# Zeros pad three small matrices of the mambas to 68 rows

## The chip, the cores and the metric

The kernel runs on one NeuronCore of a Trainium2 chip. The metric is the device time of one execution in microseconds, the median of several runs. The engines have short names in the profile: PE is the tensor engine (PEld its weight loads), DVE the vector engine, ACT the scalar engine, POOL the GpSimd engine, and SP the engine whose queue issues most of the DMA transfers. Each engine works through its own instructions in program order, and semaphores make them wait for each other.

## The reference

The program is a sequence of four layers on an image batch of 4 x 192 x 64 x 64 in float32. Layer 0 holds two mamba blocks on the same normalised input (the second sees its channels reversed), layer 1 one mamba block, followed by a depthwise convolution and an MLP. Layers 2 and 3 are a masked depthwise convolution with weights made from pooled channels, and windowed mixing with an MLP. The change touches the mambas only. Each of them computes, for every token,

```
xc, z = split(x @ in_w.T);  xc = silu(causal_conv(xc) + conv_b)
dbl = xc @ x_w.T                        # 12 + 16 + 16 = 44 values a token
dt = softplus(dbl[:12] @ dt_w.T + dt_b) # 384 channels
B, C = dbl[12:28], dbl[28:44]
h = exp(dt * A) * h + dt * xc * B       # 384 x 16 states
y = sum over states of h * C, + D * xc, times silu(z);  out = y @ out_w.T
```

There are 4096 tokens an image and 4 images. The 44 values a token, `dbl`, are what matters here: 12 of them give the step sizes `dt`, 16 are B and 16 are C.

## The kernel before

The tokens are cut into units of 512, 32 units for each mamba: 64 units in layer 0, where the two mambas alternate, and 32 in layer 1. Tiles are laid with channels on the partitions and 512 tokens along the free dimension. Float32 products are recorded as two passes each, a weight load and a matmul a pass.

A unit has a front and a scan. The front (`Mamba.front`) makes, one after the other: the input projection into `ps_in` (line 475, weights of 96 rows), the convolution as shifted diagonal matmuls into `ps_conv` (line 557, mambas of layer 0 only; layer 1 sums the taps with ACT and POOL), silu, then the x-projection into `ps_x` (line 493: three products accumulate 384 channels into 44 output partitions), a copy by ACT into the SBUF tile `dbl` (line 495), and the three products of `dt_w` with the first 12 rows of `dbl` into `ps_dt` (line 504), each evicted by ACT (line 507). Softplus follows, POOL multiplies `dt` with `xc`, and both go to DRAM, from where `load` (line 602) reads them back, each row repeated over 8 partitions.

The scan takes 12 groups of 128 (channel, state) pairs four times over. `spread` (line 609) and `spread_C` (line 625) multiply a matrix of zeros and ones with `dbl` and so repeat the rows of B and C over the partitions: each is a product with 44 contracted rows and 128 output columns, two for B and two for C a unit. ACT makes the decays `dA` (line 648), DVE or POOL the product of `dtxE` and B (line 641), DVE runs the scan (line 654), POOL multiplies with C (line 667), and PE gathers the sum over states into `y` (line 676). In the gather four products of 32 output columns each write four quarters of the partitions.

The order of the instructions on every engine is written out by a planner, `Behind`, before anything runs: the scans set the pace, and pieces of the fronts, of the norms and of the work after the scans are placed between them, by costs and dues given as constants in the code. Such a constant is not worked out from the sizes of the tiles. PSUM banks of the front rotate over two buffers, and one `dbl` is in use at a time.

Layers 2 and 3 start from the images of layer 1 and end the program; from about 8660 us on nothing but these runs.

Of the kernel before, what the change touches and what calls it, by code (L numbers as in the profile page):

```python
# [14 lines left out]
F32 = mybir.dt.float32  # L15
# [11 lines left out]
DI = 384  # L27
ND = DI // 128
NS = 16
RK = 12  # L30
HID = 768
NH = HID // 128
T = 512
# [21 lines left out]
class Pack:  # L55


    def __init__(self, parts):
        self.parts, self.arrays, self.at, self.width = parts, [], {}, 0
# [24 lines left out]
def chunked(a, p):  # L84

    a = a.reshape((a.shape[0] // p, p) + a.shape[1:])
    return np.moveaxis(a, 0, 1)
# [318 lines left out]
class Expand:  # L406
# [3 lines left out]


    def __init__(self, nc, const, spread_ap, gather_ap):
        self.spread = const.tile([RK + 2 * NS, 4, 128], F32, name="spread")
        nc.sync.dma_start(self.spread, spread_ap)
        self.gather = const.tile([128, 2, 32], F32, name="gather")
        nc.sync.dma_start(self.gather, gather_ap)


class Mamba:
# [3 lines left out]
    def __init__(  # L423
        self, nc, name, taps, ins, const, last, scan, work, psum_y, psum_a, dram, ident, ex, behind, shared=(),
        summed=False, xcs=3,
    ):

        self.behind, self.xcs, self.shared, self.summed = behind, xcs, shared, summed
        self.nc, self.name, self.taps, self.ex = nc, name, taps, ex
        self.last, self.work, self.psum_y, self.psum_a = last, work, psum_y, psum_a
        self.dram = dram
        pack, pack_ap, in_w_ap, dt_w_ap = ins
        t = const.tile([128, pack.width], F32, name=f"{name}_pack")
        nc.sync.dma_start(t, pack_ap)
        w = pack.views(t)
        self.in_w = scan.tile([CP, 2, 2 * DI], F32, name=f"{name}_in_w")
        nc.scalar.dma_start(self.in_w, in_w_ap)  # L440
        self.dt_w = scan.tile([RK, DI], F32, name=f"{name}_dt_w")
        nc.scalar.dma_start(self.dt_w, dt_w_ap)
        self.conv_b, self.dt_b, self.D = w["conv_b"], w["dt_b"], w["D"]
        self.x_w, self.out_w = w["x_w"], w["out_w"]
        self.A = scan.tile([128, NQ, 4], F32, name=f"{name}_A")
        nc.scalar.activation(self.A, w["A_log"], AF.Exp)
        nc.vector.tensor_scalar_mul(self.A, self.A, -1.0)
        self.conv_w = w["conv_w"]
        if not summed:
            self.conv = scan.tile([128, ND, taps, 128], F32, name=f"{name}_conv")  # L450
            for d in range(ND):
                for j in range(taps):
                    nc.vector.tensor_scalar_mul(
                        self.conv[:, d, j, :], ident, w["conv_w"][:, d, j : j + 1]
                    )
        if not summed:
            self.skip_w = scan.tile([128, ND, 128], F32, name=f"{name}_skip")
            for d in range(ND):
                nc.vector.tensor_scalar_mul(self.skip_w[:, d, :], ident, self.D[:, d : d + 1])
        self.halo = scan.tile([128, ND, taps if summed else taps - 1], F32, name=f"{name}_halo")  # L460
        self.state = scan.tile([128, NQ, 4], F32, name=f"{name}_state")

    def front(self, xn, first, u):


        nc, K, behind = self.nc, self.taps, self.behind
        raw = self.work.tile([128, ND, K - 1 + T], F32, name="raw", bufs=1)
        if first:
            nc.gpsimd.memset(self.halo, 0.0)
        nc.gpsimd.tensor_copy(raw[:, :, 0 : K - 1], self.halo[:, :, : K - 1])  # L470

        def projected(e):
            ps = behind.bank([128, T], "ps_in")
            for k in range(2):
                nc.tensor.matmul(  # L475
                    ps, self.in_w[:, k, bass.ts(e, 128)], xn[:, k, :], start=(k == 0), stop=(k == 1)
                )
            return ps

        def project(e, to):  # L480
            ps = projected(e)
            return behind.later(lambda: nc.scalar.copy(to, ps))  # L482

        if self.summed:
            yield from self.sum_taps(raw, projected, u)
        else:
            yield from self.convolve(raw, project, u)
        xc = u["xc"]
        nc.scalar.activation(xc, xc, AF.Silu)  # L489
        yield Piece(2.6, bank=True, wait=2 if self.summed else 4)  # L490
        ps = behind.bank([RK + 2 * NS, T], "ps_x")
        for d in range(ND):
            nc.tensor.matmul(ps, self.x_w[:, d, :], xc[:, d, :], start=(d == 0), stop=(d == ND - 1))  # L493
        dbl = u["dbl"] = self.work.tile([RK + 2 * NS, T], F32, name="dbl", bufs=1)
        h = behind.later(lambda ps=ps: nc.scalar.copy(dbl, ps))  # L495
        halves = []
        for d in range(ND):
            yield Piece(0.85, bank=True, after=[h], wait=0 if d else 3)
            if d == 0:
                dt = self.work.tile([128, ND, 1 + T if self.summed else T], F32, name="dt", bufs=1)  # L500
                dt = dt[:, :, :T]
                dtx = raw[:, :, K - 1 :]
            ps = behind.bank([128, T], "ps_dt")
            nc.tensor.matmul(ps, self.dt_w[:, bass.ts(d, 128)], dbl[:RK, :], start=True, stop=True)  # L504
            halves.append(
                behind.later(
                    lambda d=d, ps=ps: nc.scalar.activation(
                        dt[:, d, :], ps, AF.Identity, bias=self.dt_b[:, d : d + 1]
                    )
                )  # L510
            )
        yield Piece(after=halves, burst=True, act=4.1)
        nc.scalar.activation(dt, dt, AF.Softplus)  # L513
        nc.gpsimd.tensor_tensor(dtx, dt, xc, ALU.mult)  # L514
        rows = []
        for i, v in enumerate((dt, dtx)):
            yield Piece(wait=1 + i)
            r = self.dram.tile([DI, T], F32, name=("r_dt", "r_dtx")[i], bufs=3)
            nc.sync.dma_start(r.rearrange("(c p) t -> p c t", p=128), v)
            rows.append(r)  # L520
        yield Piece(1.7, bank=True, after=u["z_free"])
        u["rows"] = rows
        z = u["z"] = self.work.tile([128, ND, T], F32, name="z", bufs=2)
        made = []
        for d in range(ND):
            if d:
                yield Piece(1.7, bank=True)
            made.append(project(ND + d, z[:, d, :]))

        def silu():  # L530
            nc.scalar.activation(z, z, AF.Silu)
            u["silu"] = True
            yield Piece()

        said = Piece(after=made, burst=True, act=4.1)
        if self.summed:
            behind.add(4, silu(), said)
        else:
            yield said
            yield from silu()  # L540
# [1190 lines left out]
def scan_order(a):  # L1731

    a = a.reshape(ND, 4, 2, 16, 2, 8)
    return a.transpose(3, 5, 0, 2, 4, 1).reshape(128, NQ, 4)


def scan_matrices():
    spread = np.zeros((RK + 2 * NS, 4, 16, 8), np.float32)
    for o in range(4):
        for n in range(8):  # L1740
            spread[RK + 8 * o + n, o, :, n] = 1.0
    gather = np.zeros((16, 8, 2, 2, 16), np.float32)
    for q in range(2):
        for dd in range(16):
            gather[dd, :, q, q, dd] = 1.0
    return spread.reshape(RK + 2 * NS, 4, 128), gather.reshape(128, 2, 32)


def laid_out(inputs):

    arrays, packs = {}, {}

    def mamba(name, in_w, conv_w, conv_b, x_w, dt_w, dt_b, A_log, D, out_w):
        p = packs[name] = Pack(128)
        for n, a in (
            ("conv_w", conv_w),
            ("conv_b", conv_b),
            ("dt_b", dt_b),
            ("D", D),
            ("A_log", scan_order(A_log)),  # L1760
            ("x_w", x_w.T),
            ("out_w", out_w.T),
        ):
            p.add(n, a if n == "A_log" else chunked(a, 128))
        arrays[f"{name}_in_w"] = chunked(in_w.T, CP)
        arrays[f"{name}_dt_w"] = dt_w.T

    order = ["in_w", "conv_w", "conv_b", "x_w", "dt_w", "dt_b", "A_log", "D", "out_w"]
    m1 = [inputs[f"L0_conv_m1_{n}"] for n in order]
# [7 lines left out]

    i = {k[len("L1_conv_") :]: v for k, v in inputs.items() if k.startswith("L1_conv_")}
    mamba(
        "m",  # L1780
        i["in_proj_w"],
# [42 lines left out]
    arrays["sed"] = paired(np.moveaxis(i["w_sed"], 0, 1))[:, :2]  # L1824

    arrays["spread"], arrays["gather"] = scan_matrices()
    for n, p in packs.items():
        arrays[n] = p.array()
# [18 lines left out]
```

## Time and profile before

| | |
|---|---|
| median of 3 runs | 10563.82 us (10560.6 to 10564.75) |
| span of the profiled execution | 10559.3 us |
| PE busy | 8657.5 us, 82% of the span |
| DVE busy | 8765.6 us, 83% |
| POOL busy | 7932.4 us, 75% |
| ACT busy | 6675.7 us, 63% |
| mean granted PE clock | 0.860 |
| `ps_x` (line 493), 128 rows, 44 columns | 576 passes, 592 / 598 / 1084 ns (shortest, median, longest) |
| `ps_dt` (line 504), 12 rows, 128 columns | 576 passes, 587 / 692 / 1219 ns |
| `B` (line 609), 44 rows, 128 columns | 384 passes, 588 / 693 / 1220 ns |
| `ps_C` (line 625), 44 rows, 128 columns | 384 passes, 588 / 590 / 1220 ns |

A row of the profile names the line, engine and operation, what is written and read, and the form: "44*128 44x512" is a weight of 44 rows and 128 columns, and 44 partitions of 512 moving elements. A matmul's own duration holds its way through the array, which overlaps the next one; what a pass takes from PE is the distance between starts. The clock row gives the share of the full PE clock that was granted. In a table by stretches each column is an engine's busy time in that stretch, then the clock, the share of the DMA engines' time and their rate. In a line of waits the three numbers are the total in us, how often, and the longest.

### The profile page before, as it was taken

The numbers are of one execution on the slowest core, as the hardware profiler recorded it, in microseconds if no ns is written. First come the engines' busy times: TensorE is split into PE (matmuls) and PEld (weight loads), VectorE is DVE, ScalarE is ACT, GpSimd is POOL, SyncE is SP. The second block draws the span as 40 slices with busy tenths as digits, with TensorE's granted clock in tenths as the row PEclk, the third lists the DMA queues.
The fourth block names the chain that finished last, engine by engine and source line by source line (L and its number), as shares of the span: only waits on it lengthen the run. The fifth ranks groups of instructions, "written<-read, shape, count | busy, mean of one in ns | idle before, by whom it ended". The sixth has DMA issues, their size and how long they took to land. (4 is left out here: it accounts for less than half of the span.)

```text
span 10559.3 us, 96732 instructions
## 1 busy us (share of the span) xinstructions
PE 8657.5 (82%) x30648; PEld 3478.9 (33%) x30648; DVE 8765.6 (83%) x7569; ACT 6675.7 (63%) x9690; POOL 7932.4 (75%) x3712
## 2 busy tenths in 40 slices
PE   6777777877877777787668888888888996889898
PEld 2222222322322222222223333333333333545555
DVE  7999999999999999999878887887888876555552
ACT  5776777667777667767456676776776653434443
POOL 6999999999999999999778887888888861101100
PEclk7888888888888888888668898998998987999999
DMA  6666666666666666666555554555555543122110
GB/s 163 183 187 180 178 183 186 178 181 188 182 179 183 183 181 180 185 182 179 143 143 148 134 153 131 152 138 143 141 149 135 149 109 74 42 56 59 41 41 19
DMA packets 969559, 1515.09 MB, mean 143 GB/s; under 512 B 244346, under 2 KB 277150, under 8 KB 968534
## 3 DMA queue, kind: packets, MB, share of 16 engines
q1 hardware_dynamic: 968190, 1505.85, 53.5%
q8 instruction: 243, 3.98, 0.2%
q10 hardware_dynamic: 856, 3.05, 0.1%
q14 instruction: 270, 2.21, 0.1%
HBM read 1295.45 MB, written 213.12 MB: 143 GB/s over the span
## 5 line engine op out<-in xcount | busy, mean ns | idle before, releaser
L654 DVE TENSOR_TENSOR_SCAN h<-dA,m_state,h 128x512 f32<-128x512 f32 x3328 | 4041.4, 1266 | 269.8 <-ACT dA L648 207.8
L648 ACT ACTIVATE dA<-dtE,m_A 128x512 f32<-128x512 f32 x4608 | 3101.1, 686 | 1217.6 <-DVE h L654 925.4
L667 POOL TENSOR_TENSOR h<-h,C 128x2048 f32<-128x2048 f32 x832 | 3768.3, 4529 | 71.3 <-ACT C L629 4.0
L641 DVE TENSOR_TENSOR h<-dtxE,B 128x2048 f32<-128x2048 f32 x832 | 1881.7, 2262 | 74.5 <-DMA dtxE<-r_dtx 68.1
L654 DVE TENSOR_TENSOR_SCAN h_apart<-dA,m_state,h_apart 128x512 f32<-128x512 f32 x1280 | 1551.2, 1262 | 199.9 <-ACT dA L648 190.0
L641 POOL TENSOR_TENSOR h_apart<-dtxE,Bs 128x2048 f32<-128x2048 f32 x320 | 1475.5, 4611 | 35.2 <-ACT dA L648 16.2
L667 POOL TENSOR_TENSOR h_apart<-h_apart,C 128x2048 f32<-128x2048 f32 x320 | 1449.7, 4530 | 25.8
L676 PE MATMUL y<-h,gather 128*32 128x512 f32 x6656 | 1040.1, 701 | 486.9 <-POOL h L667 311.5
L1382 POOL TENSOR_TENSOR d<-d,rs 128x512 f32<-128x512 f32 x64 | 86.3, 1348 | 1594.7 <-DVE rs L1381 1573.1
L475 PE MATMUL ps_in<-xT,m_in_w 96*128 96x512 f32 x1536 | 910.1, 742 | 247.9 <-ACT o L918 160.5
L557 PE MATMUL ps_conv<-raw,m_conv 128*128 128x512 f32 x1536 | 732.0, 610 | 8.3 <-ACT raw L482 7.1
L475 PEld LDWEIGHTS ps_in<-xT,m_in_w 96*128 96x128 f32 x1536 | 356.8, 242 | 835.6 <-issue 378.0
L1131 PE MATMUL ps_dw<-strip,dw 96*96 96x512 f32 x1152 | 596.7, 669 | 1.1 <-ACT x L1140 0.9
L504 PE MATMUL ps_dt<-dbl,m_dt_w 12*128 12x512 f32 x576 | 427.7, 847 | 165.9 <-ACT dbl L495 102.5
L676 PE MATMUL y<-h_apart,gather 128*32 128x512 f32 x2560 | 397.8, 698 | 178.7 <-POOL h_apart L667 169.9
L493 PE MATMUL ps_x<-xc,m_pack 128*44 128x512 f32 x576 | 361.8, 779 | 193.1 <-ACT xc L489 178.5
L676 PEld LDWEIGHTS y<-h,gather 128*32 128x32 f32 x6656 | 140.2, 115 | 1122.6 <-issue 574.3
L475 PE MATMUL ps_in<-xn,m_in_w 96*128 96x512 f32 x768 | 403.1, 660 | 114.8 <-ACT z L482 61.7
L1547 PE MATMUL sed_ps<-xn,sed 64*128 64x256 f32 (+3 forms) x2944 | 487.3, 405 | 7.0 <-DVE y L1566 7.0
L514 POOL TENSOR_TENSOR raw<-dt,xc 128x1536 f32<-128x1536 f32 x96 | 325.0, 3386 | 222.9 <-ACT dt L513 180.7
L395 PE MATMUL ps_o<-hid,t 128*96 128x512 f32 x768 | 418.5, 684 | 70.5 <-ACT C L629 63.7
L648 ACT ACT_TABLE_LOAD x345 | 442.6, 1283 | 14.7 <-DMA dtE<-r_dt 8.6
(200 smaller groups left out, 12103.5 us busy)
## 6 DMA issues: line engine op xcount, KB each, us to landing
dtE<-r_dt SPq DMA_DIRECT2D x2304, 256.0 KB, 5.2
dtxE<-r_dtx SPq DMA_DIRECT2D x2304, 256.0 KB, 4.3
r_dt<-dt SPq DMA_DIRECT2D x96, 768.0 KB, 4.0
r_dtx<-raw SPq DMA_DIRECT2D x96, 768.0 KB, 6.5
x<-x SPq DMA_DIRECT2D x64, 384.0 KB, 3.6
img<-x SPq DMA_DIRECT2D x28, 512.0 KB, 8.6
xt<-in_x SPq DMA_DIRECT2D x32, 384.0 KB, 5.4
x<-o SPq DMA_DIRECT2D x32, 384.0 KB, 4.2
```

The lines of the kernel that those rows point to most:

```text
L395: nc.tensor.matmul(ps, self.w2[:, m, bass.ts(k, CP)], h[:, m, :], start=(m == 0), stop=(m == NH - 1),)
L475: nc.tensor.matmul(ps, self.in_w[:, k, bass.ts(e, 128)], xn[:, k, :], start=(k == 0), stop=(k == 1))
L493: nc.tensor.matmul(ps, self.x_w[:, d, :], xc[:, d, :], start=(d == 0), stop=(d == ND - 1))
L504: nc.tensor.matmul(ps, self.dt_w[:, bass.ts(d, 128)], dbl[:RK, :], start=True, stop=True)
L557: nc.tensor.matmul(ps, self.conv[:, d, j, :], raw[:, d, j : j + T], start=(j == 0), stop=(j == K - 1))
L641: engine.tensor_tensor(h, u["rows", k // 2, 1], u[B, k % 2].unsqueeze(1).broadcast_to([128, 4, T]), ALU.mult)
L648: self.nc.scalar.activation(dA, u["rows", k // 2, 0][:, j, :], AF.Exp, scale=self.A[:, k, j : j + 1])
L654: self.nc.vector.tensor_tensor_scan(h[:, j, :], u.pop(("dA", k, j)), h[:, j, :], self.state[:, k, j : j + 1], ALU.mult, ALU.add,)
L667: nc.gpsimd.tensor_tensor(h, h, u["C", k % 2].unsqueeze(1).broadcast_to([128, 4, T]), ALU.mult)
L676: self.nc.tensor.matmul(u["ys"][32 * j : 32 * j + 32, :], self.ex.gather[:, i // 2, :], h[:, j, :], start=(i == 0), stop=(i == 3 and self. ...
L1131: nc.tensor.matmul(ps, dw[:, k, j, :], s[:, k, dy : dy + rows, dx : dx + HW], start=(j == 0), stop=(j == 8),)
L1547: nc.tensor.matmul(out, sed[p, int(h is not None), i ^ position(k, s), cols], xn[b, g][p, c, :], start=group(t) not in begun, stop=left[gr ...
```

## The change

Zero columns are added to the x-projection's weights, so that `ps_x` and `dbl` have 68 rows instead of 44, of which the last 24 are zero. Zero rows are added to `dt_w` (12 to 68) and to the spread matrices (44 to 68). The products for `dt` now contract all 68 rows of `dbl`; those for B and C do so as well. The results are the same numbers. The number and order of the instructions in the code stay.

```diff
+KX = 68
...
-        self.spread = const.tile([RK + 2 * NS, 4, 128], F32, name="spread")
+        self.spread = const.tile([KX, 4, 128], F32, name="spread")
...
-        self.dt_w = scan.tile([RK, DI], F32, name=f"{name}_dt_w")
+        self.dt_w = scan.tile([KX, DI], F32, name=f"{name}_dt_w")
...
-        ps = behind.bank([RK + 2 * NS, T], "ps_x")
+        ps = behind.bank([KX, T], "ps_x")
...
-        dbl = u["dbl"] = self.work.tile([RK + 2 * NS, T], F32, name="dbl", bufs=1)
+        dbl = u["dbl"] = self.work.tile([KX, T], F32, name="dbl", bufs=1)
...
-            nc.tensor.matmul(ps, self.dt_w[:, bass.ts(d, 128)], dbl[:RK, :], start=True, stop=True)
+            nc.tensor.matmul(ps, self.dt_w[:, bass.ts(d, 128)], dbl, start=True, stop=True)
...
-    spread = np.zeros((RK + 2 * NS, 4, 16, 8), np.float32)
+    spread = np.zeros((KX, 4, 16, 8), np.float32)
...
-            ("x_w", x_w.T),
+            ("x_w", np.pad(x_w.T, ((0, 0), (0, KX - x_w.shape[0])))),
...
-        arrays[f"{name}_dt_w"] = dt_w.T
+        arrays[f"{name}_dt_w"] = np.pad(dt_w.T, ((0, KX - RK), (0, 0)))
```

## The prediction

> **What bounds the kernel now.** I read the page first, then busy time by stage, the waits, the tensor engine's timeline, and last the clock. In the page's slices PE is well filled, DVE nearly full for two thirds of the time, and the clock granted to PE is below full almost throughout.
>
> ```profile
> span 10559.3 us, 96732 instructions
> ...
> PE   6777777877877777787668888888888996889898
> ...
> DVE  7999999999999999999878887887888876555552
> ...
> PEclk7888888888888888888668898998998987999999
> ```
>
> The scans stop near 8650 us; the first block (two mambas) ends near 5250 us, the second (one mamba) near 8660 us. The busy time of those stretches and of what follows:
>
> ```profile
> core 0: us, PE busy (x) PEld busy (x) DVE busy (x) ACT busy (x) POOL busy (x), PEclk, DMA share, GB/s
> 60.00:5250.00 5190.00, 4045.14 (x13123) 1441.01 (x13121) 4980.03 (x3819) 3585.85 (x5499) 4902.59 (x2083) 0.82 0.67 180
> 5250.00:8660.00 3410.00, 2962.25 (x9073) 1058.48 (x9073) 2775.59 (x2248) 2309.29 (x3096) 2814.79 (x1401) 0.88 0.53 141
> ```
>
> In the first block DVE is idle for only 5190 - 4980 = 210 us: scans bound it, and PE has slack. In the second DVE idles 634 us and PE is the fullest engine (87%). The waits of the second block say who is late:
>
> ```profile
> ACT x L1140 <- PE ps_dw L1131: 163.8, 58, 4.9
> DVE h L654 <- ACT dA L648: 150.1, 150, 7.0
> DVE h_apart L654 <- ACT dA L648: 137.3, 79, 6.1
> ACT C L629 <- PE ps_C L625: 125.3, 34, 7.3
> DVE strip L1102 <- PE ps_out L1093: 124.4, 60, 5.4
> ACT dt L507 <- PE ps_dt L504: 47.7, 32, 4.2
> ACT dbl L495 <- PE ps_x L493: 39.7, 12, 8.5
> ```
>
> ACT runs strictly in order. While it waits for PE to finish ps_dw, ps_C, ps_dt or ps_x, the decays dA (L648) stand behind it, and scans wait for those. Following releases back from the last scan of each block, in the manner of the page's chain, I find PE work on 929 of the first block's 5180 us (POOL 2029, DVE 1490), but on 1719 of the second's 3310.
>
> **What a switch of array form costs.** The products that the change touches stand between others like this (weight loads on PEld, at full clock):
>
> ```profile
> 1529.88 0.19 PEld L557 LDWEIGHTS ps_conv<-raw,m_conv 128*128 128x128 f32 x1 [0.24 <-issue]
> 1530.83 0.29 PEld L609 LDWEIGHTS B<-dbl,spread 44*128 44x128 f32 x2 [0.76 <-DVE h L654]
> 1531.88 0.30 PEld L557 LDWEIGHTS ps_conv<-raw,m_conv 128*128 128x128 f32 x2 [0.76 <-ACT xc L562]
> 1532.42 0.19 PEld L557 LDWEIGHTS ps_conv<-raw,m_conv 128*128 128x128 f32 x1 [0.24 <-issue]
> ```
>
> Inside one form loads are 0.43 us apart and fully hidden behind the matmul before. At B (44 rows) the load comes late, and so again on the way back. B's two passes take 1531.88 - 1530.83 = 1.05 us of PE instead of 2 x 0.43. Taking all back-to-back starts: 428 ns between passes of one form; 519 to 522 into another form (+90), and then 533 between its first two passes, since the first 128-column load is not hidden (+105). Together 195 ns a switch. At half clock 853, about 985 and 1015: 132 + 162 = 294 ns. Passes of 96 rows cost no switch beside 128 rows. Of 68 to 95 rows or columns no instruction exists here; I take them as the 96-row ones.
>
> **What decides the clock.** The clock record knows two values, 1.0 and 0.5, in steps of 3.413 us. These are four such steps:
>
> ```profile
> 2769.14:2772.55 3.41, 3.41 (x11) 0.54 (x9) 3.31 (x3) 0.69 (x1) 3.33 (x3) 0.50 1.06 254
> 2772.55:2775.97 3.42, 2.16 (x6) 0.50 (x2) 3.42 (x4) 3.07 (x5) 3.34 (x3) 0.50 1.07 252
> 1495.97:1499.38 3.41, 3.41 (x5) 1.35 (x4) 3.04 (x3) 3.38 (x4) 3.14 (x2) 0.50 0.35 134
> 1499.38:1502.80 3.42, 2.33 (x6) 0.76 (x4) 3.42 (x4) 2.80 (x5) 3.34 (x3) 1.00 1.03 280
> ```
>
> Both the first and the third have PE busy throughout at half clock. The first is ps_dt (12 rows) and a gather, and the next step stays at 0.50; the third is mostly ps_in (96 rows), and the next is at 1.00. So I summed, step by step, streaming time x rows / 128 (each of the gather's four simultaneous column tiles as a quarter). In the first block, of 252 half-clock steps with a sum above 0.705, 234 are followed by full clock, and of the 280 below none is. Of 756 full-clock steps above 0.365, 754 stay full; of 232 below, none. Rows decide, not mere busy time. That is a fit to this one trace.
>
> **What the Trainium skill says.** "TensorEngine Tiling (Array Packing)", Key Properties, says that changing the tiling mode drains the engine; the trace agrees, with the price above. "TensorE: Matmul & The Clock Gate", LDWEIGHTS, says that load time goes with columns, not rows; the trace agrees (about 182 ns for 12 and for 44 rows at 128 columns, 115 for 44 columns). The same page, Part 1, has a 3413 ns activity window and the two clocks; the trace agrees on both, but here activity counts rows.
>
> **The change part by part.** Instruction order stays, so nothing is moved past a queue and no wait is added; the 68-row product reads the dbl that it already waited for.
>
> Switches: in the order of matmuls 3910 neighbours differ in form; with L493, L504, L609 and L625 as whole-array ones 3210 do. The gather (32 columns) stays, so those beside it remain. Of the 700, 440 are in the first block and 260 in the second. At 195 or 294 ns each, and only the load's part where PE was idle before, that frees 85 and 55 us of PE. On the two chains lie 23 and 47 us of it.
>
> Clock: dt's rows go from 12 to 68, B's and C's from 44 to 68, with the same streaming time. With the new row sums 50 of the first block's 532 half-clock steps would become full, and 20 of the second's 240. The chains hold 442 and 534 us of PE at half clock; halving their share gives 442 x 50/532 / 2 = 21 us and 534 x 20/240 / 2 = 22 us. Bounds: 48 and 8 steps if zero rows do not count, 121 and 67 if 68 rows count as 128; 0 if the fit is chance. I take the plain row count.
>
> So the chains get shorter by 44 us (first) and 69 us (second). Not all of it passes on. In the first block DVE and POOL (4903 of 5190 us) are full next to each chain piece; waits of scans for dA, the route by which PE reaches them, are 110 us in all: I pass a third, 15 us. In the second, scan waits and direct PE waits of DVE make up most of 634 us idle: I pass 0.6, 41 us. Both shares are choices; 0 and 1 are the bounds. What is late next is the scans themselves, then POOL.
>
> Costs: ps_x loads 68 columns instead of 44. Between 115 ns (44) and 182 (128) that is some 19 ns, bare only after a gather: under 2 us of PE. Its copy into dbl takes 570 ns for 44 partitions, and copies of 128 partitions take 582: at most 12 ns x 96, about 1 us of ACT, beside work. Loads grow by 84 KB per dt_w, 36 KB per pack, 48 KB per spread matrix: 288 KB before the first xt lands on the SP queue (12.60 us), 168 KB at the second block's start. At the 260 GB/s of those stretches that is 1.1 + 0.65 us, on the path: 2 us. No extra bank is needed: 68 x 512 is one.
>
> Sum against the profiled execution: 10559.3 - 15 - 41 + 2 = 10505 us of span. The median (10563.8) lies 4.5 us above, for what surrounds the span and run-to-run spread: 10510 us.
>
> **The rivals.** (1) The clock counts the whole tile: 68 rows like 128. Then 121 and 67 steps turn, chain gains of 50 and 75 us in place of 21 and 22; at the same shares some 42 us more, 10468. For it: the switches do go by tile. Against: the 96-row work fits better as 0.75. (2) Hidden anyway: each chain has a near equal beside it, and ACT, no longer held by PE, is held by DVE (dA waits 793 us for h in the first block). 15 us or less survive: 10555. (3) Slower: PE's work bunches up and leaves emptier steps behind, so the clock falls more often. Place: the second block, where a half-clock step costs the chain 534 / 240 / 2 = 1.1 us. It needs 54 / 1.1 = 49 more half-clock steps there (240 to 289) to cancel the gain, 20 more to be slower by 0.2%; I price it at 10600, some 80 more such steps. Against: no work leaves PE and rows only grow. (4) 68 is no whole-array form, switches stay: only the clock gain passes on (7 + 13 us), about 10546; the forms seen (96 as 128) speak against it, and it counts within (2).
>
> **Numbers.** Forecast 0.55, (1) 0.12, (2) with (4) 0.20, (3) 0.13. About 0.2% (21 us) is what a measurement of this kernel can tell from no change. Faster 0.67, same 0.20, slower 0.13. The forecast's own range is 10455 (all 113 us pass) to 10542. Taking in (2) and the near parts of (1) and (3): 10450 to 10580.
>
> **What would show it.** Right: B's two passes between conv passes 0.86 us instead of 1.05; some 3210 switches; fewer half-clock steps, clock near 0.84 in the first block and 0.90 in the second; ACT's waits for ps_C, ps_dt and ps_dw lower; three quarters of the gain between 5250 and 8660 us. Wrong: switches unchanged, a lower clock, or PE freed while scans wait as before.

## The result: 107 us faster, all of it in the second block

The change takes 10455.11 us (median, 10453.6 to 10458.36), against 10562.21 us for the kernel before in the same comparison: a ratio of 0.990, 95% interval 0.9888 to 0.9912, or 107 us. The forecast was 10510 us, some 54 us faster. The sign was right, and so was the second block as the place where both mechanisms act; the size was half of what came, and the part forecast for the first block did not come.

The same three rows of the page, after the change:

```profile
span 10456.3 us, 96737 instructions
...
PE   6777777777777777777658898888898886989898
...
DVE  7999999999999999999958888888888876555552
...
PEclk8888888888888888888768899999999997999999
```

DVE's row looks as it did, and PE's clock has more nines in the last half. A split at the first and the last scan of each block says where the time went. In this table "start" is the time to the first scan, "between" the gap between the two blocks' scans, "rest" what follows the last scan (from the scans' times in the trace; us):

| kernel | start | first block | between | second block | rest | span |
|---|---|---|---|---|---|---|
| before | 76.4 | 5150.1 | 98.4 | 3325.6 | 1908.8 | 10559.3 |
| the change | 80.0 | 5149.2 | 104.9 | 3216.1 | 1906.1 | 10456.3 |

The second block gained 109.5 us, the first nothing, and 10 us were lost at the start and between the blocks. The busy times of the two blocks, first before, then after (columns as in the prediction: length, busy time and instructions of PE, PEld, DVE, ACT and POOL, PE's clock, DMA share, GB/s):

```profile
76.40:5226.50 5150.10, 4025.19 (x13036) 1428.28 (x13036) 4976.81 (x3813) 3581.38 (x5491) 4895.72 (x2078) 0.83 0.67 180
5324.90:8650.50 3325.60, 2911.36 (x8985) 1039.02 (x8986) 2766.75 (x2221) 2284.46 (x3064) 2798.78 (x1390) 0.89 0.53 142
```

```profile
80.00:5229.20 5149.20, 3923.70 (x13036) 1428.42 (x13036) 4977.07 (x3813) 3577.63 (x5491) 4885.31 (x2078) 0.83 0.68 180
5334.10:8550.20 3216.10, 2806.49 (x8985) 1042.43 (x8986) 2763.76 (x2221) 2284.72 (x3064) 2800.91 (x1390) 0.91 0.55 147
```

PE's busy time falls by about 100 us in each block. In the first it turns into idle time of PE; in the second the block gets shorter by it. DVE's work is the same to 3 us in both.

The switches behave as the prediction said. The weight loads around a B product, after the change:

```profile
1532.71 0.19 PEld L558 LDWEIGHTS ps_conv<-raw,m_conv 128*128 128x128 f32 x1 [0.24 <-issue]
1533.14 0.19 PEld L610 LDWEIGHTS B<-dbl,spread 68*128 68x128 f32 x1 [0.24 <-DVE h L655]
1533.57 0.19 PEld L610 LDWEIGHTS B<-dbl,spread 68*128 68x128 f32 x1 [0.24 <-issue]
1534.00 0.19 PEld L558 LDWEIGHTS ps_conv<-raw,m_conv 128*128 128x128 f32 x1 [0.24 <-issue]
```

All loads are 0.43 us apart: B's two passes take 1534.00 - 1533.14 = 0.86 us, no longer 1.05, and 68 rows do count as the whole array. In the order of matmuls 3210 neighbours differ in form, exactly the count forecast (3910 before).

The waits of the second block after the change (what waits, for what; total us, times, longest):

```profile
DVE strip L1103 <- PE ps_out L1094: 130.6, 60, 5.4
ACT C L630 <- PE ps_C L626: 114.3, 33, 7.0
DVE h L655 <- ACT dA L649: 104.3, 133, 7.2
ACT x L1141 <- PE ps_dw L1132: 95.6, 57, 4.3
DVE h_apart L655 <- ACT dA L649: 81.2, 67, 3.8
```

The scans' waits for dA fell from 150.1 + 137.3 to 104.3 + 81.2 us, 102 us less, close to the block's gain. The largest fall among ACT's waits for PE is that for ps_dw, 163.8 to 95.6 us. The change doesn't touch ps_dw; but of its 1152 passes 170 started at half clock before, and 58 do now.

### The profile page after: what moved, and what is told of

It reads as the page before. It is cut to its first block, busy times and chain, and to the rows that moved or that the text cites. A ratio compares the mean times of both kernels' runs of the same rounds, so it can differ in the third digit from the quotient of the medians.

```text
span 10456.3 us, 96737 instructions
## 1 busy us (share of the span) xinstructions
PE 8434.2 (81%) x30648; PEld 3477.0 (33%) x30648; DVE 8762.8 (84%) x7569; ACT 6672.4 (64%) x9690; POOL 7925.1 (76%) x3712
## 5 line engine op out<-in xcount | busy, mean ns | idle before, releaser
L476 PE MATMUL ps_in<-xT,m_in_w 96*128 96x512 f32 x1536 | 951.6, 772 | 340.2 <-ACT o L919 213.4
L494 PE MATMUL ps_x<-xc,m_pack 128*68 128x512 f32 x576 | 374.8, 802 | 213.3 <-ACT xc L490 198.6
L1132 PE MATMUL ps_dw<-strip,dw 96*96 96x512 f32 x1152 | 544.8, 620 | 1.3 <-ACT x L1141 0.9
L505 PE MATMUL ps_dt<-dbl,m_dt_w 68*128 68x512 f32 x576 | 379.3, 761 | 167.6 <-ACT dbl L496 101.3
```

The lines of the kernel that those rows point to most:

```text
L476: nc.tensor.matmul(ps, self.in_w[:, k, bass.ts(e, 128)], xn[:, k, :], start=(k == 0), stop=(k == 1))
L505: nc.tensor.matmul(ps, self.dt_w[:, bass.ts(d, 128)], dbl, start=True, stop=True)
L1132: nc.tensor.matmul(ps, dw[:, k, j, :], s[:, k, dy : dy + rows, dx : dx + HW], start=(j == 0), stop=(j == 8),)
```

## The experiments

Each run is set against the kernel before on the same chip. The diffs are against the change, and "..." marks what is left out of them.

**64 rows: the clock without the switches.** The question was how the gain splits between switches and clock. With 64 in place of 68 the form of the three products stays narrow, and so do all 3910 switches, while the rows rise almost as far. Each triple is columns of the x-projection's weights, rows of `dt_w`, rows of the spread matrices; K0 is for the first block, K1 for the second.

```diff
-KX = 68
+K0 = (64, 64, 64)
+K1 = (64, 64, 64)
...
```

> All three matrices padded to 64 rows or columns instead of 68. Counted in the trace of before, this leaves all 3910 switches of array form where they are, while the row count of the dt, B and C products (64) stays near that of the change (68). Theory 'both' (in the second block some 55 us of the change's 107 us come from switches that are gone, some 55 us from a higher clock through more rows): 40 to 60 us faster than before, 10505 to 10525 us, and near 174 to 190 half-clock steps in the second block instead of 220. Rival 'switches alone' (the clock only follows from a busier engine): within 15 us of before. Rival 'clock alone' (a switch costs nothing on the path): 90 us or more faster, as the change itself.

It took 10498.49 us, ratio 0.9942 (0.9925 to 0.9958), 62 us faster, with 3910 switches in its trace. They still cost what they did: B's two passes take 1532.94 - 1531.89 = 1.05 us, with 64 rows as with 44:

```profile
1530.94 0.19 PEld L560 LDWEIGHTS ps_conv<-raw,m_conv 128*128 128x128 f32 x1 [0.24 <-issue]
1531.89 0.29 PEld L612 LDWEIGHTS B<-dbl,spread 64*128 64x128 f32 x2 [0.76 <-DVE xc L701]
1532.94 0.30 PEld L560 LDWEIGHTS ps_conv<-raw,m_conv 128*128 128x128 f32 x2 [0.76 <-ACT xc L565]
```

So more rows at unchanged switches, and the clock that follows from them, are worth 62 us, and the 45 us up to the change's 107 come from the switches, given that clock. That is a little past what was expected. Both rivals fall. The switches without the rows were not measured: a form of more than 64 rows has the rows too. The second block took 3260.8 us, 64.8 less than before; its half-clock steps of 3.413 us were 172, against 220 before and 174 in the change, just below the range expected.

What a turned step (one that is at full clock and was at half before) is worth shows in one unit of the second block, the twentieth, where this kernel gained 10.9 us (113.45 to 102.59 us between first scans). The steps of the clock record that hold its dt products, before:

```profile
7353.25:7356.66 3.41, 2.63 (x9) 0.71 (x6) 3.13 (x4) 1.28 (x3) 2.79 (x2) 1.00 1.06 252
7356.66:7360.07 3.41, 3.41 (x5) 1.11 (x6) 0.68 (x1) 0.68 (x1) 2.59 (x2) 0.50 0.42 97
7360.07:7363.49 3.42, 3.42 (x5) 0.70 (x3) 0.10 (x1) 1.55 (x3) 2.10 (x1) 0.50 0.00 0
7363.49:7366.90 3.41, 3.41 (x5) 1.25 (x5) 3.41 (x3) 3.36 (x5) 0.00 (x0) 0.50 0.00 0
7366.90:7370.31 3.41, 3.41 (x11) 0.49 (x9) 3.41 (x3) 3.37 (x4) 1.62 (x1) 0.50 0.22 88
```

The same place with 64 rows:

```profile
7315.47:7318.88 3.41, 2.63 (x6) 0.78 (x7) 3.31 (x3) 1.70 (x3) 3.33 (x2) 1.00 1.05 273
7318.88:7322.29 3.41, 3.41 (x6) 0.97 (x4) 2.48 (x3) 0.29 (x1) 3.25 (x4) 0.50 1.05 272
7322.29:7325.71 3.42, 3.42 (x9) 1.15 (x8) 1.41 (x2) 2.86 (x5) 3.42 (x1) 1.00 0.10 28
7325.71:7329.12 3.41, 3.41 (x15) 0.93 (x14) 3.41 (x4) 3.38 (x4) 0.50 (x1) 1.00 0.00 0
```

Before, four steps in a row run at half clock (the column of the clock, third from the end) although PE is busy for all of the 3.41 us in each. DVE then runs dry: 0.68 and 0.10 us of work in two of them. The last dt product, with 12 rows, lies in the second of the four and keeps its row sum at 0.40. With 64 rows one step at half clock is left. But what turned here is not the step with that product. The first half-clock step, in which only ps_dw (96 rows) runs in either kernel, has a row sum of 0.72 before and 0.75 with 64 rows. In the kernel before, ps_dw starts 0.1 us ahead of that step, and the delay that follows its switch of form falls into it; with 64 rows ps_dw starts 0.6 us ahead, and the delay is over. Only the second is followed by full clock (both lie above the 0.705 of the prediction's fit; the first is one of its misses). So in this unit the rows worked by way of a shifted timetable, which the prediction's count could not see.

**The second block alone, the first block alone.** Did the first block contribute anything?

```diff
-        self.dt_w = scan.tile([KX, DI], F32, name=f"{name}_dt_w")
+        self.kx = K1 if summed else K0     # K1 for the second block
+        self.dt_w = scan.tile([self.kx[1], DI], F32, name=f"{name}_dt_w")
...
# second block alone: K0 = (44, 12, 44), K1 = (68, 68, 68); first alone: the reverse
```

> Padding to 68 in the mamba of the second block alone; the two mambas of the first block as before. Theory (the first block is bound by the scans on DVE and gains nothing): the whole gain stays, 100 to 115 us faster than before, 10448 to 10462 us, since the first block also saves its longer loads of some 3 us. Rival (the first block contributes a third of the gain that the prediction gave it, 15 us, and the trace of the change hid that): 85 to 95 us faster.

> Padding to 68 in the two mambas of the first block alone. Theory (bound by DVE): 0 to 5 us slower than before, for the longer loads at the start, although 440 switches are gone and PE is less busy there by some 100 us. Rival (part of it passes, as predicted): 10 to 20 us faster.

The second block alone took 10448.38 us, ratio 0.9893 (0.9878 to 0.9908), 112 us faster: the whole gain and a few us more, about as many as its gap between the blocks is shorter than the change's (98.8 against 104.9 us). The first block alone took 10564.12 us, ratio 1.0003 (0.9994 to 1.0012): no difference. Its two blocks:

```profile
78.40:5226.20 5147.80, 3882.36 (x13036) 1398.72 (x13036) 4981.14 (x3813) 3580.32 (x5491) 4891.99 (x2078) 0.83 0.68 180
5325.80:8653.50 3327.70, 2915.05 (x8985) 1040.05 (x8986) 2766.64 (x2221) 2285.05 (x3064) 2799.90 (x1390) 0.89 0.54 142
```

PE works 143 us less in the first block than before (4025 to 3882), and the block is 2 us shorter. DVE is busy for 4981 of 5148 us. The scans' waits there, in the kernel before and then in this one:

```profile
DVE h L654 <- ACT dA L648: 57.7, 126, 7.1
DVE h_apart L654 <- ACT dA L648: 52.6, 35, 2.5
DVE h L641 <- DMA dtxE<-r_dtx: 19.8, 1, 19.8
DVE h L641 <- PE y L676: 5.8, 14, 0.5
```

```profile
DVE h L657 <- ACT dA L651: 73.8, 153, 8.3
DVE h_apart L657 <- ACT dA L651: 20.6, 32, 2.2
DVE h L644 <- DMA dtxE<-r_dtx: 19.6, 1, 19.6
DVE h L644 <- PE y L679: 16.8, 30, 0.7
```

They wait for dA 94 us in all, against 110 us before, and for y 17 us in place of 6. So most of the little that PE gives back comes out at another place: the rival "hidden anyway" holds for this block.

**128 rows.** If rows drive the clock, more of them should help. The padding need not be zeros in the x-projection: the weights that lie behind its own can be read as further columns. Rows 44 to 127 of `dbl` are then products with other weights, finite numbers, and they meet zero rows of `dt_w` and of the spread matrices. Nothing is left out.

```diff
-        self.x_w, self.out_w = w["x_w"], w["out_w"]
+        self.out_w = w["out_w"]
+        at, n = pack.at["x_w"][0], RK + 2 * NS
+        self.x_w = [t[:, at + n * d : at + n * d + self.kx[0]] for d in range(ND)]
...
-            ("x_w", np.pad(x_w.T, ((0, 0), (0, KX - x_w.shape[0])))),
+            ("x_w", x_w.T),
...
# dbl, dt_w and the spread matrices with 128 rows
```

> 128 rows in all mambas: the x-projection's weights are read 128 columns wide out of the packed weights, so that rows 44 to 127 of dbl are products with other weights, finite numbers that meet zero rows of dt_w and of the spread matrices. Switches as in the change (3210), rows of the dt, B and C products 128 instead of 68. Theory 'both', with rows deciding the clock: in the trace of before 67 half-clock steps of the second block would turn full with 128 rows against 20 with 68, so the clock part at least doubles: 150 to 200 us faster than before, 10360 to 10410 us. If the clock looks at the array's form alone (68 rows already count as 128), or at switches: as the change, within 20 us of 10455.

It took 10434.7 us, ratio 0.988 (0.9865 to 0.9895): 126 us faster than before, so 19 us better than the change's 107. That is short of the 150 to 200 us, and a hair outside the 20 us around 10455 of the other reading: neither range held. The change and this kernel once more, both on one chip:

> The change once more, beside the kernel with 128 rows on one chip: 100 to 115 us faster than before, 10445 to 10460 us.

> 128 rows everywhere once more. If its 20 us over the change are real (6 us in the second block, the rest at the end of the first and between the two): 120 to 130 us faster than before and 12 to 25 us faster than the change on the same chip. If chance: within 8 us of the change.

The change took 10453.94 us (0.9899, 0.9882 to 0.9915) and 128 rows 10435.01 us (0.9884, 0.9869 to 0.9898). The medians are again 19 us apart. The intervals of the two ratios overlap, but the times themselves don't (10449.5 to 10456.3 against 10434.0 to 10441.3 us). The clock did rise with the rows, at the same forms: between the first and the last scan, half-clock steps fell from 173 to 162 in the second block and from 530 to 460 in the first, in these two runs. So the clock does not look at the form alone. But the second block gained only 5.6 us from it (3215.9 to 3210.3), the first 6.4 us, and the gap between them went from 104.7 to 97.7 us.

To see whether the first block's part was chance, the same for the second block only, with the first as before:

> 128 rows in the second block's mamba alone, the first block as before. The second block took 3210 us with 128 rows and 3216 with 68, and the first block ended 6 us earlier with 128 rows, which is either the rows there or chance. If rows help the first block too: 5 to 15 us slower than with 128 rows everywhere, 10440 to 10450 us. If its start and end were chance: as that, 10430 to 10437 us.

It took 10438.27 us, ratio 0.9883 (0.9868 to 0.9898), 4 us from 128 rows everywhere and between the two ranges expected. Its first block took 5146.9 us. The kernel with 68 rows in the second block alone has the same first block and took 5151.3 us for it, so chance alone makes 4.4 us; with 128 rows there it took 5144.2 and 5141.8 us. A gain of the first block from 128 rows is at most a few us, and not settled. Either version is faster than the change.

**One part alone.** dt at 68 rows with the spread matrices at 44, and the reverse (both with the x-projection at 68 columns):

```diff
# dt alone: K0 = K1 = (68, 68, 44);  spread matrices alone: K0 = K1 = (68, 12, 68)
-            nc.tensor.matmul(ps, self.dt_w[:, bass.ts(d, 128)], dbl, start=True, stop=True)
+            nc.tensor.matmul(ps, self.dt_w[:, bass.ts(d, 128)], dbl[: self.kx[1], :], start=True, stop=True)
...
-        self.nc.tensor.matmul(B, self.ex.spread[:, o, :], u["dbl"], start=True, stop=True)
+        self.nc.tensor.matmul(B, self.ex.spread[:, o, :], u["dbl"][: self.kx[2], :], start=True, stop=True)
```

> x-projection and dt_w padded to 68, the spread matrices at 44 rows. Counted in the trace of before, 109 of the second block's 255 switches go (0.66 us a unit at full clock), and dt's rows rise, B's and C's don't. Theory 'each part adds up' (clock some 62 us as with 64 rows, of which dt has most, switches by their number): 62 x 0.8 + 45 x 109/255 = 69 us faster, 10492 us, and a steady unit of the second block at some 101.7 us. Rival 'the pace is locked to the clock's step' (a steady unit measured 102.40 us with and without 64 rows, 30.0 steps of 3.413 us, and 100.69, 29.5 steps, in the change): steady units stay at 102.4, and the gain is that of the 64 rows or a little less, 10500 to 10510 us.

> x-projection and spread matrices padded to 68, dt_w at 12 rows. 175 of the second block's 255 switches go (1.07 us a unit); the row sums rise less (9 half-clock steps would turn in the second block, against 14 with dt alone). 'Each part adds up': 62 x 0.3 + 45 x 175/255 = 50 us faster, 10511 us, a steady unit at 101.2 us. Rival 'locked': steady units at 102.4 or 100.7 us and nothing between.

dt alone took 10526.24 us, ratio 0.9966 (0.9952 to 0.998), 34 us faster; the spread matrices alone 10528.6 us, ratio 0.9969 (0.9956 to 0.9982), 31 us faster. Together that is 65 us where the change gives 107, and both of my expectations missed for either. What the parts do to a unit of the second block is no sum: the times between first scans, from the traces (us, five units in a row of each, away from the start of an image):

```
before            102.4  102.4  102.4  102.4  102.4
64 rows           102.5  102.5  102.4  102.4  102.4
dt alone          106.1  106.0  101.9  106.1  106.0
spread alone      105.4  107.7  101.4  105.2  107.6
the change        100.5  100.9  100.5  100.9  100.5
```

102.40 us is 30.0 of the clock's steps of 3.4133 us; the change's pairs of 201.4 us are 59.0 of them; dt alone comes back after three units of 314.0 us, 92.0 steps. Whole images, of eight units each, come back in whole steps as well: in the last two images of these five kernels the first scan of a unit follows that of the same unit one image earlier after 246.0, 241.0, 245.0, 245.0 and 237.0 steps (the block's last unit aside). So the units have settled into patterns that repeat against the clock's steps. My reading is that removing part of the PE work can lead into a pattern with a bad step in it. It is a reading: no run shifts the steps against the loop with the work left alone, and the kernel with 128 rows, the fastest, shows no whole number (237.3 to 237.7).

**More PE work.** If so, a little more PE work should not cost what it takes either.

```diff
-            nc.tensor.matmul(ps, self.dt_w[:, bass.ts(d, 128)], dbl, start=True, stop=True)
+            for _ in range(2 if self.summed and d == 0 else 1):
+                nc.tensor.matmul(ps, self.dt_w[:, bass.ts(d, 128)], dbl, start=True, stop=True)
```

> The change with one product more in the second block: the first dt product of a unit is made twice, two passes, 0.86 us of PE a unit at full clock. Chain theory (PE work ahead of the decays passes whole): 32 x 0.86 = 27 us slower than the change, about 10482 us, steady units at 101.5 us. Rival 'locked': steady units stay at 100.7 us and the kernel is within 8 us of the change, or they jump to 102.4 and it is 50 us slower.

It took 10538.89 us, ratio 0.9981 (0.9972 to 0.999): only 21 us faster than before, so 84 us behind the change, for 27 us of work. Its second block:

```profile
5329.60:8628.10 3298.50, 2894.37 (x9047) 1070.11 (x9048) 2765.69 (x2221) 2283.43 (x3064) 2800.05 (x1390) 0.89 0.54 143
```

3298.5 us against 3216.1, with the clock back at 0.89 and 213 half-clock steps instead of 174. The additive chain fails, and so does the plain lock: most units take 102.1 us, 0.3 us less than 30 steps, so each starts 0.3 us earlier against the steps than the one before, and in between come units of 107 to 114 us.

## Why the prediction was right in kind and wrong in size

The step that failed is the clock term of the second block: 22 us on its chain, of which 13 us were to reach the time, and 64.8 us came. Two more terms of the sum were off: the share passed on for the switches there (28 us, 44.7 came), and the first block (15 us, none came). Against the prediction's own steps:

- **Where.** Right. "Three quarters of the gain between 5250 and 8660 us" was too cautious: all of it is there.
- **Switches.** The price (1.05 us for B's two passes, 0.86 without switches) and the count (700) hold in the trace; 255 of them are in the second block, near the 260 counted. On the second chain lay 47 us of them, of which I passed 0.6, 28 us; the difference between 64 and 68 rows in the second block is 3260.8 - 3216.1 = 44.7 us. At the clock of the 64-row kernel the share passed was close to one; the parts run alone warn against taking it as a fixed share.
- **Clock, second block.** This is the term that was mis-sized most. I counted 20 turned half-clock steps, 22 us on the chain, 13 us passed. The run with 64 rows measured 64.8 us for the block, with 48 half-clock steps fewer: more than twice the steps, and 1.35 us for each, where 1.1 us on the chain and 0.6 of that in the time were forecast. The count laid the new row sums over the old timetable, step by step, and so held the timetable fixed. In the unit shown it was a shift of the timetable that turned a step, and the next ones then filled with 96-row work at full clock, so that four became one. How many of the 48 came that way was not counted.
- **First block.** Wrong: a third of 44 us was to pass, none did (1.0003, 0.9994 to 1.0012, alone). The share was a choice without a measurement behind it. Nor is the chain there a firm measure: followed again by the page's rule from the block's last scan it holds 713 us of PE before, not 929, and 1327 us after the change, though the block is as long (in the second block 1663 us before, near the 1719 of the prediction). DVE idles for 173 us there, and with less PE work it still does. The 50 turned steps of the count are not to be seen either: the traces have 525, 541 and 527 half-clock steps in a first block as before, and 503, 530 and 509 with 68 rows.
- **Costs.** Estimated 2 us; 10 us were lost at the places where I had put them, but not for the reason I gave. The first scan is 3.6 us later, the gap between the blocks 6.5 us longer. The larger loads don't explain the start: with 128 rows everywhere they are larger still, and the first scan comes at 75.9 and 77.3 us. In the gap the load of the spread matrix is issued late, before and after:

```profile
5246.34 0.37 SPq L923 DMA_DIRECT2D x<-o  x1
5246.76 0.44 SPq L414 DMA_DIRECT2D spread<-in_spread  x1
```

```profile
5249.05 0.37 SPq L924 DMA_DIRECT2D x<-o  x1
5256.12 0.28 SPq L415 DMA_DIRECT2D spread<-in_spread  x1
```

  Before, it was issued 0.42 us after that store, now 7.07 us after it, and the pack queued behind it is late too. With the second block alone at 68 rows, and the same loads there, the gap is 98.8 us, so the bytes are not the reason. Why SP waits was not found.
- **Rival (1), the whole tile counts.** It came nearest in time (10468), for the wrong reason: 128 rows give still fewer half-clock steps than 68. In the change's own trace, too, the row rule tells the step after a half-clock one in 97.6% of the cases with 68 rows, in 92.0% with 128 written in their place (60 to 8660 us; in the repeat of the change 94.5% and 93.2%).
- **Rivals (2) and (3).** Hidden for the first block, not for the second. The clock falling instead of rising did not happen with the change, but it is what one product more brought back in the last experiment.
- **The end of the range.** With all 113 us of both chains passed, the sum is 10563.8 - 113 + 2 = 10453 us (the prediction has 10455). The measured 10455.11 us lies there by luck: the first block gave nothing of its 44 us, and the second 109.5 us where 69 were on its chain.

In sum, in us of span: 64.8 + 44.7 in the second block, 0.9 in the first, 2.7 after the scans, less 3.6 and 6.5: the 103.0 by which the two spans differ.

## What to carry to other kernels

Price a change to the tensor engine block by block. Here the block where that engine is the fullest gave more than what lay on its chain, and the block where another engine is busy 97% of the time, DVE, gave nothing; shares of 0.6 and a third were wrong on both sides. Where PE's clock goes up and down in steps, count rows of the weights and not only busy time, and remember that a count on the old timetable misses the steps that turn because the timetable moves. In a loop whose period settles on a multiple of such a step, small savings need not add: run the parts and the whole.

## What the runs showed of the hardware that I had not expected

- The clock's steps follow streaming time x rows of the weight, zero rows included. The rule was fitted to the trace of before, and it holds, less sharply in some, in the others. In the change, from 60 us to the first scan of the second block, all of 788 full-clock steps above 0.365 stayed full and none of 229 below did; of 241 half-clock steps above 0.705, 228 were followed by full clock, of the 286 below none. For half-clock steps above 0.705 it is weaker in the repeat of the change (228 of 264) and in the first run with 128 rows (229 of 273). With the best threshold for each, rows tell 99.6 to 99.8% of the full-clock steps of before, the change and the 64-row kernel, and busy time without rows 95.8 to 96.5%.
- Zero weight rows count. The plainest sign is the 64-row kernel itself, which adds nothing but zero rows and columns at the same forms and loses 48 half-clock steps in the second block. Leaving those rows out of the sum in its trace (12 for dt, 44 for B and C) lowers the share of full-clock steps told rightly from 99.6% to 95.4% (60 to 8660 us). Whether zeros among the moving data count is open: without them the share is 99.1%.
- The repeating patterns of units against the 3.413 us steps: 30.0 steps a unit before, 59.0 for two units after, whole numbers for an image in five kernels, and 84 us lost for 27 us of added work.
